# Half of some steps' exponentials on VectorE, in a convolution and attention kernel whose ScalarE and TensorE are both full

## The chip, the cores and the metric

The kernel runs on one core of one Trainium2 chip. A core has five engines that run their own instruction streams in order and meet through semaphores: TensorE (PE in the profile; its weight loads are PEld), VectorE (DVE), ScalarE (ACT), GpSimd (POOL) and SyncE (SP), whose queue issues nearly all DMAs here. The metric is the device time of one execution in microseconds, as the median of several runs. Differences below about 0.2% can't be told from no change.

## What is computed

An image batch of 4 x 64 x 64 x 128 in fp32 goes through two layers. Layer 0 is a gated block: ELU, a 3x3 convolution, a second one with a gate, and a strictly causal attention over the 4096 pixels of an image. Layer 1 is a transformer block on the same 4096 tokens: full attention with 16 heads of 8 channels, a gated feed-forward part, and a mixture of 8 experts of which two are used per token. The part that fills the time is layer 1's attention:

```python
scores = jnp.einsum('bqhd,bkhd->bhqk', q, k)      # 4 images x 16 heads x 4096 x 4096
probs = jax.nn.softmax(scores.astype(jnp.float32), axis=-1).astype(q.dtype)
attn = jnp.einsum('bhqk,bkhd->bqhd', probs, v).reshape(bsz, seqlen, DIM)
```

That is 4 x 16 x 4096 x 4096, or 1.07 billion exponentials. The kernel takes no maximum away before the exponential (it bounds the scores instead, and has a second, general path that runs only where the bound is exceeded); the row sums come from a column of ones beside the values.

## The kernel before, in words

**Attention steps.** Heads are worked on in 4 groups (g) of 4, queries in 8 chunks (c) of 512, keys in 32 tiles (kt) of 128. One `attention_step` (L776) is one group, one query chunk and one key tile. Its first half, `scores()`, puts four matmuls of 512 columns into two PSUM tiles of 1024 (`s`, from a pool of three) and has ScalarE take the exponential of each into an SBUF tile `e` of 1024, from a ring of eight. Its second half, `values(es)`, multiplies the four parts of the two `e` tiles with the values and adds to the one PSUM accumulator `acc`. An image has 4 x 8 x 32 = 1024 such steps, the four images 4096. A `Segment` is a run of key tiles for one group and chunk, mostly all 32; in the first image some are split, so that work may begin while keys are still being made. At a segment's end DVE copies `acc` to SBUF (`at`).

**First steps.** Layer 0's attention uses the same kind of step with two exponentials, `first_step` (L701): 36 an image. Together these are 4240 steps with 8480 exponentials of about 1024 columns.

**Fillers.** Everything else (convolutions, projections, feed-forward, experts) is written as generators that yield after each small piece, with the piece's TensorE time: `first_attention` and `convolutions` for the next image, `second_operands`, and `last_part` after the attention of a chunk. They use one PSUM tile of one bank (`m`, from a pool of one), which DVE empties after each piece.

**Order.** The order of each engine's instructions is the order in which the program writes them: `InOrder` (L91) ties every instruction to the one before it on its engine. The main loop (from L1188) makes one turn per step: it writes the scores of the next step (`do_step`), adds a rate to a credit in microseconds of TensorE, lets one filler piece in while the credit is positive (`insert`), and then writes values until two steps are left undone (`finish(2)`). So the values of a step stand two turns after its scores. The rate is the fillers' remaining TensorE time by the steps left for it. In the first two turns of a segment no filler is let in (`quiet`). Before the loop, `run_alone` works through the first image's preparation, and after it through what is left of the fillers, both with the `s` tiles in place of `m` (`alone`).

All instructions carry the line of the recording helper (L105 before), so the profile is read by the names of the tiles: `s<-qx,f_kx` are a step's scores, `e<-s` an exponential, `acc<-e,vg` values, and `m<-...` fillers.

```python
        credit = min(0.7, credit + rate)
        if waiting or credit > 0.0 and not quiet[0] or urgent and not held[0]:
            credit -= insert()
        finish(2)
```

Of the kernel before, what the change touches and what calls it, by code (L numbers as in the profile page):

```python
# [9 lines left out]
FP = mybir.dt.float32  # L10
FR = mybir.dt.float32r
AF = mybir.ActivationFunctionType
ALU = mybir.AluOpType
AX = mybir.AxisListType

P = 128
C = 128
IMG = 64
N = IMG * IMG
NT = N // P  # L20
QB = 512
# [70 lines left out]
    return np.concatenate(list(parts.values()), axis=1), where  # L92


class InOrder:


    def __init__(self, tc, engine):
        self._tc, self._engine, self._last = tc, engine, None

    def __getattr__(self, name):
        op = getattr(self._engine, name)

        def call(*args, **kw):
            made = op(*args, **kw)  # L105
            if self._last is not None:
                after = mybir.DependencyInfo(mybir.DependencyClass.NoSync, mybir.DependencyReason.DATA)
                self._tc.add_manual_dep(made.ins, self._last, after, reason="as written")
            self._last = made.ins.name
            return made  # L110

        return call
# [3 lines left out]
def fast_path(ctx: ExitStack, tc: tile.TileContext, a: dict, where: dict, out: bass.AP, verdict):  # L116
# [10 lines left out]

    const = ctx.enter_context(tc.tile_pool(name="f_const", bufs=1))
    big = ctx.enter_context(tc.tile_pool(name="f_big", bufs=1))
    ep = ctx.enter_context(tc.tile_pool(name="f_ep", bufs=8))  # L130
    wk = ctx.enter_context(tc.tile_pool(name="f_wk", bufs=2))
    sm = ctx.enter_context(tc.tile_pool(name="f_sm", bufs=2))
    dram = ctx.enter_context(tc.tile_pool(name="f_dram", bufs=2, space=bass.MemoryType.DRAM))
# [15 lines left out]

    def chunk(tag, name=None):  # L150
        return wk.tile([P, QB], FP, tag=tag, bufs=CHUNKS.get(tag, 1), name=name or tag)

    def small(name, dims):
        return sm.tile([P, *dims], FP, tag=name, name=name)
# [64 lines left out]
    seen = const.tile([P, 4, B], FP, name="f_seen")  # L219


    steps_in, undone, fillers, urgent = [], [], [], []
    held, turn = [False], [0]

    def do_step(step):
        scores, values = step
        undone.append((values, scores()))

    def finish(leave):
        while len(undone) > leave:  # L230
            values, es = undone.pop(0)
            values(es)

    def advance(part):

# [67 lines left out]
    def spread(eng, taps, u_all):  # L303
# [22 lines left out]
            yield 0.0, "stop"  # L326
        spread_of.append(u_all)

    def row_terms(band):
        r = wk.tile([P, 4, 8, IMG + 2], FP, tag="r", bufs=1, name="r")  # L330
        for i, (x, y, op) in enumerate(SUMS):
            pool.tensor_tensor(r[:, i], band[:, x : x + 15 : 2, :], band[:, y : y + 15 : 2, :], op)
        return r
# [272 lines left out]
    def second_operands(b, st):  # L606

        c, d = st.second, st.d
        cols = slice(c * QB, (c + 1) * QB)
        if c == 0:  # L610
            tops_of[b] = small("top1", [2, 2, NQ]), small("topv1", [NQ])
        top1, top_v1 = tops_of[b]
        t, at = st.ready[c]
        cols = slice(c * QB, (c + 1) * QB)


        for pair in range(2):
            ps = bank()[:, : 2 * (C + 1)].rearrange("p (k c) -> p k c", k=2)
            for i in range(2):
                k = 2 * pair + i  # L620
                product(ps[:, i, :], at[:, k * P : (k + 1) * P], w3f)
            rs = small("rs0", [2])
            dve.tensor_scalar(rs, ps[:, :, C], 1e-35, None, ALU.add)
            dve.reciprocal(rs, rs)
            for i in range(2):
                tk = by_k(t)[:, 2 * pair + i, :]
                dve.scalar_tensor_tensor(tk, ps[:, i, :C], rs[:, i : i + 1], tk, ALU.mult, ALU.add)
            if pair == 1:
                st.read += 1
            yield 0.46, "stop"  # L630
        h = chunk("h")
        layernorm(t, h)
        for _ in range(2):
            yield 0.0, "stop"
        sp.dma_start(out=d["t"][c], in_=t)
        sp.dma_start(out=d["h"][c], in_=h)
        yield 0.0, "stop"

        ps = bank()
        transposed(h, ps)  # L640
        yT = chunk("yT")
        dve.tensor_copy(yT, ps)
        yield 0.6, "stop"
        def terms(i, w):

            ps = bank()
            yield from halves(ps, w, yT)
            u = chunk("u")
            two = wk.tile([P, 2, QB], FP, tag="two", bufs=1, name="two")
            dve.tensor_copy(u, ps)  # L650
            dve.tensor_copy(two[:, 0, :].bitcast(FR), u)
            dve.tensor_tensor(two[:, 1, :].bitcast(FR), u, two[:, 0, :], ALU.subtract)
            dve.tensor_reduce(top1[:, i, :, c], two, AX.X, ALU.max, apply_absolute_value=True)
            yield 0.46, "stop"
            if i == 0:
                for y in range(2):
                    sp.dma_start(out=d["q"][c][:, y], in_=two)
            else:
                sp.dma_start(out=d["k"][:, :, cols], in_=two)

        yield from terms(0, wq1)

        ps = bank()
        by_g = ps.rearrange("p (g k s) -> p k g s", g=NG1, k=4)
        for k in range(4):
            product(by_g[:, k], yT[:, k * P : (k + 1) * P], wv1)
            if k == 1:
                yield 0.46, "held"
        vc = wk.tile([P, 4 * NH1, 1 + HD1], FP, tag="vc", bufs=1, name="vc")
        pool.memset(vc[:, :, 0:1], 1.0)  # L670
        dve.tensor_copy(vc[:, :, 1:], ps.rearrange("p (f s) -> p f s", s=HD1))
        dve.tensor_reduce(
            top_v1[:, c : c + 1], vc.rearrange("p f s -> p (f s)"), AX.X, ALU.max, apply_absolute_value=True
        )
        yield 0.46, "stop"
        sp.dma_start(
            out=d["v"][:, :, c].rearrange("g p s -> p g s"),
            in_=vc.rearrange("p (g f) s -> p g (f s)", g=NG1),
        )
        yield from terms(1, wk1)  # L680
        if c == NQ - 1:

            tops2, tops = small("tops2", [2, 2]), small("tops", [2])
            dve.tensor_reduce(tops2, top1, AX.X, ALU.max)
            dve.tensor_tensor(tops, tops2[:, :, 0], tops2[:, :, 1], ALU.add)
            s2 = seen[:, 2, b : b + 1]
            dve.tensor_tensor(s2, tops[:, 0:1], tops[:, 1:2], ALU.mult)
            dve.tensor_scalar(s2, s2, 1e30, None, ALU.min)
            dve.tensor_reduce(seen[:, 3, b : b + 1], top_v1, AX.X, ALU.max)
        st.second += 1  # L690
# [10 lines left out]
    def first_step(c, r, qx0, sums, found):  # L701
# [47 lines left out]
                dve.tensor_copy(at, sums[0])  # L749
                found.append(at)  # L750

        return scores, values


    def keys(d, g, quarter, place):
# [17 lines left out]
        )  # L773
        return vg

    def attention_step(b, seg, kt, place, qx, vg, part):  # L776
        g, c = seg.g, seg.c

        def scores():
            ss, es = [s_tile(), s_tile()], []  # L780
            for j in range(NSLOT):
                r = slice(j * SLOT, (j + 1) * SLOT)
                pe.matmul(
                    ss[j // 2][:, (j % 2) * QB : (j % 2 + 1) * QB],
                    lhsT=kx[r, place * P : (place + 1) * P].bitcast(FR),
                    rhs=qx[r, :].bitcast(FR),
                    start=True,
                    stop=True,
                )
            for s in ss:  # L790
                e = e_tile()
                act.activation(e, s, AF.Exp)
                es.append(e)
            return es

        def values(es):
            for j in range(NSLOT):
                pe.matmul(
                    acc[j * SLOT : j * SLOT + 1 + HD1, :],
                    lhsT=vg[:, kt // 4, kt % 4, j, :],  # L800
                    rhs=es[j // 2][:, (j % 2) * QB : (j % 2 + 1) * QB],
                    start=kt == seg.lo,
                    stop=kt == seg.hi - 1,
                )
# [8 lines left out]
                else:  # L813
                    sp.dma_start(out=scratch[b]["p"][g, c], in_=at)

        return scores, values

    def by_token(b, g, c, at):

# [301 lines left out]
    def stream():  # L1121
# [16 lines left out]
        for at, seg in enumerate(plan):  # L1138
# [13 lines left out]
            for kt in range(seg.lo, seg.hi):  # L1152
# [3 lines left out]
                if seg.lo > 0 and kt == seg.lo + 4:  # L1156

                    part.append(chunk("part"))
                    sp.dma_start(out=part[0], in_=scratch[seg.b]["p"][seg.g, seg.c])
                yield attention_step(seg.b, seg, kt, 8 * seg.place(kt // 8) + kt % 8, qx, vg, part)  # L1160
                if follower and follower not in ahead and follower.ready():
                    bring(follower)
                if kt % 8 == 7:
# [24 lines left out]
    credit, waiting = 0.0, False  # L1188
    while True:
        turn[0] += 1  # L1190
        if steps_in:
            do_step(steps_in.pop(0))
        else:
            step = next(steps, False)
            if step is False:
                break
            waiting = step is None
            if waiting:
                finish(0)
            else:  # L1200
                do_step(step)
        b = now[0]
        if batches[b].second == NQ and len(batches) == b + 1 and b + 1 < B:
            Batch(b + 1)
# [3 lines left out]
        if batches[b].second == NQ:  # L1208
            within = steps_left[b] - 40 if b + 1 < B else min(steps_left[b] - 40, 160)
            rate = sum(us for _, us in fillers) / max(1, within)  # L1210
        credit = min(0.7, credit + rate)
        if waiting or credit > 0.0 and not quiet[0] or urgent and not held[0]:
            credit -= insert()
        finish(2)
    finish(0)
    while urgent:
        if held[0]:
# [722 lines left out]
```

## Time and profile before

| | before |
|---|---|
| median of 3 runs | 8293.93 us (8293.24 to 8297.26) |
| the profiled execution | 8302.43 us |
| its span, first to last instruction | 8300.7 us |
| granted TensorE clock, mean | 0.985 |
| TensorE busy (matmuls) | 8073.1 us, 97% |
| ScalarE busy | 7915.4 us, 95% |
| VectorE busy | 2557.3 us, 31% |
| GpSimd busy | 708.5 us, 9% |
| DMA, share of 16 engines | about 11% |
| first and last exponential | 129.5 and 8222.2 us |

A line of the profile's groups has the line, engine and operation, output and input by the program's names, shape, count, then busy time and the mean duration of one, then the idle time of the engine before these instructions and what ended it. Matmuls are pipelined and their ends are modelled, so a busy TensorE is not TensorE at its peak: what it needs is read from the distance between the starts of groups that follow each other without a wait. Likewise an exponential's mean of 1087 ns is longer than the distance between two of them.

### The profile page before, as it was taken

The numbers are of one execution on the slowest core, as the hardware profiler recorded it, in microseconds if no ns is written. First come the engines' busy times: TensorE is split into PE (matmuls) and PEld (weight loads), VectorE is DVE, ScalarE is ACT, GpSimd is POOL, SyncE is SP. The second block draws the span as 40 slices with busy tenths as digits, with TensorE's granted clock in tenths as the row PEclk, the third lists the DMA queues.
The fourth block names the chain that finished last, engine by engine and source line by source line (L and its number), as shares of the span: only waits on it lengthen the run. The fifth ranks groups of instructions, "written<-read, shape, count | busy, mean of one in ns | idle before, by whom it ended". The sixth has DMA issues, their size and how long they took to land.

```text
span 8300.7 us, 173662 instructions
## 1 busy us (share of the span) xinstructions
PE 8073.1 (97%) x73713; PEld 2576.8 (31%) x73713; DVE 2557.3 (31%) x5278; ACT 7915.4 (95%) x8699; POOL 708.5 (9%) x597
## 2 busy tenths in 40 slices
PE   5899999999999999999999999999999999999998
PEld 3223222223333332333333333233333333332333
DVE  7333122223322223333322222333333223221223
ACT  1799999999999999999999999999999999999996
POOL 5101111000000002111000000211000000000000
PEclk7899999999999999999999999999999999999998
DMA  1222001101100001001010000101111111111110
GB/s 56 70 70 66 19 27 36 36 27 49 41 23 14 21 18 32 22 30 47 33 38 11 27 15 19 30 27 39 42 37 40 33 39 42 38 33 34 59 55 30
DMA packets 239541, 295.99 MB, mean 36 GB/s; under 512 B 81731, under 2 KB 153891, under 8 KB 238755
## 3 DMA queue, kind: packets, MB, share of 16 engines
q1 hardware_dynamic: 234739, 283.03, 10.6%
q8 instruction: 580, 9.50, 0.5%
q10 hardware_dynamic: 4016, 1.77, 0.1%
q14 instruction: 206, 1.69, 0.1%
HBM read 185.12 MB, written 99.61 MB: 34 GB/s over the span
## 4 chain that ended last, share of the span: by engine, by line
PE 87%; issue 7%; DVE 3%; ACT 1%; POOL 1%; DMA 1%; SPq 0%; ACTq 0%; POOLq 0%; DVEq 0%
PE acc L105 41%; PE s L105 28%; PE m L105 18%; ACT e L105 1%; DVE h L105 1%; DVE added L105 0%; DMA nt<-d_a 0%; DVE t L105 0%; POOL v L105 0%; DMA f_kx<-d_k 0%; POOL rs L105 0%; DVE two L105 0%; DMA xe<-in_x_dram 0%; DVE at L105 0%; DVE by_e L105 0%
## 5 line engine op out<-in xcount | busy, mean ns | idle before, releaser
L105 ACT ACTIVATE e<-s 128x1024 f32<-128x1024 f32 x8480 | 7842.5, 1087 | 133.4 <-PE s L105 124.3
L105 PE MATMUL acc<-e,vg 128*9 128x512 f32 x32768 | 4337.9, 595 | 1.7 <-DVE at L105 1.7
L105 PE MATMUL s<-qx,f_kx 32*128 32x512 f32 (+1 forms) x16960 | 2817.2, 495 | 46.5 <-ACT e L105 30.9
L105 PEld LDWEIGHTS s<-qx,f_kx 32*128 32x128 f32 (+1 forms) x16960 | 1128.1, 182 | 4046.7 <-ACT e L105 3788.7
L105 PEld LDWEIGHTS acc<-e,vg 128*9 128x9 f32 x32768 | 711.1, 90 | 784.0 <-issue 446.5
L105 PE MATMUL m<-v,f_wino 128*32 128x256 f32 x5328 | 431.5, 397 | 6.0 <-DVE t L105 3.5
L105 DVE TENSOR_TENSOR by_e<-m,gate 128x512 f32<-128x512 f32 x244 | 168.8, 692 | 725.7 <-PE m L105 725.7
L105 POOL TENSOR_TENSOR v<-r 128x1024 f32<-128x1024 f32 x128 | 248.5, 1947 | 1180.2 <-PE m L105 1159.9
L105 POOL TENSOR_TENSOR rs<-ve,f_minus_half 128x4 f32<-128x4 f32 x64 | 65.2, 1019 | 2997.6 <-DVE ve L105 2957.3
L105 PE MATMUL m<-f_we,y2T 128*32 128x256 f32 x3904 | 311.8, 391 | 2.3 <-DVE nt L105 2.3
L105 DVE COPY sd<-m 128x512 f32<-128x512 f32 x166 | 114.9, 692 | 570.8 <-PE m L105 570.8
L105 DVE COPY at<-acc 128x512 f32<-128x512 f32 x130 | 89.9, 692 | 555.8 <-PE acc L105 555.8
L105 DVE TENSOR_REDUCE added<-by_e 128x128 f32<-128x1024 f32 x128 | 255.3, 1995 | 4.4
L105 POOL TENSOR_TENSOR t<-t,h 128x512 f32<-128x512 f32 x32 | 40.9, 1277 | 2443.6 <-DVE h L105 2443.6
L105 PE MATMUL m<-hT,f_fw 128*32 128x256 f32 (+1 forms) x2728 | 236.1, 391 | 0.0
L105 DVE TENSOR_TENSOR t<-m,sums 128x256 f32<-128x256 f32 x126 | 53.5, 425 | 435.1 <-PE m L105 435.1
L105 DVE TENSOR_TENSOR t<-m,t 128x512 f32<-128x512 f32 x62 | 42.9, 692 | 455.6 <-PE m L105 455.6
L105 DVE SCALAR_TENSOR_TENSOR h<-m,h 128x512 f32<-128x512 f32 (+1 forms) x93 | 64.2, 690 | 372.9 <-ACT th L105 249.1
L105 DVE COPY h<-m 128x512 f32<-128x512 f32 (+1 forms) x93 | 64.2, 690 | 317.9 <-PE m L105 317.9
L105 PEld LDWEIGHTS m<-v,f_wino 128*32 128x32 f32 x5328 | 106.6, 109 | 173.5 <-issue 144.6
L105 PE MATMUL m<-e,f_v 128*32 128x512 f32 (+2 forms) x1128 | 152.2, 585 | 0.0
L105 DVE TENSOR_TENSOR e<-e,f_consts 128x128 f32<-128x128 f32 x128 | 30.2, 296 | 321.5 <-ACT e L105 321.5
(259 smaller groups left out, 3775.8 us busy)
## 6 DMA issues: line engine op xcount, KB each, us to landing
f_kx<-d_k SPq DMA_DIRECT2D x139, 512.0 KB, 4.0
qx<-d_q SPq DMA_DIRECT2D x152, 256.0 KB, 2.8
d_q<-two SPq DMA_DIRECT2D x64, 512.0 KB, 3.6
vg<-d_v SPq DMA_DIRECT2D x32, 576.0 KB, 4.2
d_k<-two SPq DMA_DIRECT2D x32, 512.0 KB, 3.4
d_v<-vc SPq DMA_DIRECT2D x32, 288.0 KB, 2.8
xe<-in_x_dram SPq DMA_DIRECT2D x32, 256.0 KB, 2.9
xt<-in_x_dram SPq DMA_DIRECT2D x32, 256.0 KB, 3.7
```

The source lines that it names most:

```text
L105: made = op(*args, **kw)
```

## The change

In some steps, called late here, the second of the two score tiles is not given to ScalarE. DVE takes it out of PSUM as z = s x log2(e) + a shift and makes 2 to that power: in two halves of 512 columns, each by adding a large constant (which leaves the whole part in the low bits), subtracting to get the fraction, a polynomial of degree five in it, a shift of the whole part into the exponent's place, and a product. These are 17 DVE instructions a late step: one of 1024 columns, four of 512 with one tensor, twelve of 512 with two. The first tile's exponential stays on ScalarE. The late step has tiles of its own (`ea`, `z`, `t`, one each; `q` shares the place of `part`), and the ring of `e` goes from eight tiles to six.

A step is late if no other one is in work, its segment begins at key tile 0, and it is the third of the segment's steps or later but not one of the last seven (`2 <= kt <= seg.hi - 8`). The instructions of the polynomial are not written at once. `InOrder` counts an estimated load for DVE (0.15 us and 1.06 ns a column for each instruction), the loop takes 1.84 us from it each turn (0.92 in a late step's), and `settle(1.5)` at the turn's end writes polynomial instructions while the load is under 1.5. The late step's values are written a turn or more after its last polynomial instruction, at the earliest three turns after its scores, in addition to the ordinary values of that turn. Before the last values of a segment all that is left is written at once (`settle(None)`). The credit for fillers gets 0.92 in a late step's turn, and loses 0.97 when its values are written.

To make room, `vc` (values on their way to DRAM) takes the place of `two` in the first image and of `r` (GpSimd's row terms of the convolutions) in the others.

In the built program 307 steps of 4096 are late, so 8173 exponentials are left to ScalarE in the loop. Of the fillers, one more expert round falls after the loop.

```diff
@@ InOrder
+        self.load = 0.0
...
+            sizes = [int(np.prod(ap.shape[1:])) for ap in (*args, *kw.values()) if hasattr(ap, "shape")]
+            self.load += 0.15 + 1.06e-3 * max(sizes, default=0)
@@ fast_path
-    ep = ctx.enter_context(tc.tile_pool(name="f_ep", bufs=8))
+    ep = ctx.enter_context(tc.tile_pool(name="f_ep", bufs=6))
...
     def do_step(step):
-        scores, values = step
-        undone.append((values, scores()))
+        scores, values, late = step
+        es = scores()
+        if late is None:
+            undone.append((values, es))
+        else:
+
+            slow.append((values, es, late, turn[0]))
...
+    def settle(limit):
+
+        if not slow:
+            return 0.0
+        values, es, todo, since = slow[0]
+        if not todo and (limit is None or turn[0] > since + 2):
+            slow.pop(0)
+            values(es)
+            return 0.97
+        while todo and (limit is None or dve.load < limit):
+            todo.pop(0)()
+        if limit is None:
+            return settle(None)
+        return 0.0
+
+    def powers(z):
+
+        todo = []
+        for h in range(2):
+            zh = z[:, h * QB : (h + 1) * QB]
+            t, q = late_tile("t"), chunk("part", "q")
+            todo.append(lambda t=t, zh=zh: dve.tensor_scalar(t, zh, MAGIC, None, ALU.add))
+
+            todo.append(
+                lambda t=t, zh=zh: dve.scalar_tensor_tensor(zh, t, MAGIC, zh, ALU.subtract, ALU.subtract)
+            )
+            todo.append(lambda q=q, zh=zh: dve.scalar_tensor_tensor(q, zh, POLY[4], zh, ALU.add, ALU.mult))
+            for k in (3, 2, 1):
+                todo.append(
+                    lambda q=q, zh=zh, k=k: dve.scalar_tensor_tensor(q, q, POLY[k], zh, ALU.add, ALU.mult)
+                )
+            bits = t.bitcast(mybir.dt.int32)
+            todo.append(lambda bits=bits: dve.tensor_scalar(bits, bits, 23, None, ALU.logical_shift_left))
+            todo.append(
+                lambda t=t, q=q, zh=zh: dve.scalar_tensor_tensor(zh, q, POLY[0], t, ALU.add, ALU.mult)
+            )
+        return todo
@@ second_operands
-        vc = wk.tile([P, 4 * NH1, 1 + HD1], FP, tag="vc", bufs=1, name="vc")
+        room = wk.tile([P, 2 * QB], FP, tag="two", bufs=1, name="vc") if b == 0 else row_tile()
+        vc = room[:, : 4 * NH1 * (1 + HD1)].rearrange("p (f s) -> p f s", s=1 + HD1)
@@ attention_step
+            if late is not None:
+                e, z = late_tile("ea", 1024), late_tile("z", 1024)
+                act.activation(e, ss[0], AF.Exp)
+                dve.tensor_scalar(z, ss[1], LOG2E, SHIFT, ALU.mult, ALU.add)
+                late.extend(powers(z))
+                return [e, z]
...
         def values(es):
+            if kt == seg.hi - 1:
+                settle(None)
@@ stream
+                late = [] if not slow and seg.lo == 0 and 2 <= kt <= seg.hi - 8 else None
@@ main loop
         turn[0] += 1
+        begun, spare = len(slow), 0.0
...
+        if len(slow) > begun:
+            spare = 0.92
+        dve.load = max(0.0, dve.load - 1.84 + spare)
...
-        credit = min(0.7, credit + rate)
+        credit = min(0.7, credit + rate) + spare
         if waiting or credit > 0.0 and not quiet[0] or urgent and not held[0]:
             credit -= insert()
         finish(2)
+        credit -= settle(1.5)
```

## Prediction

> **What bounds the kernel now.** I read the page's busy shares first, then the work by stage, then the order in time within one attention step, then the waits.
>
> ```profile
> span 8300.7 us, 173662 instructions
> PE 8073.1 (97%) x73713; PEld 2576.8 (31%) x73713; DVE 2557.3 (31%) x5278; ACT 7915.4 (95%) x8699; POOL 708.5 (9%) x597
> ...
> L105 ACT ACTIVATE e<-s 128x1024 f32<-128x1024 f32 x8480 | 7842.5, 1087 | 133.4 <-PE s L105 124.3
> L105 DVE COPY at<-acc 128x512 f32<-128x512 f32 x130 | 89.9, 692 | 555.8 <-PE acc L105 555.8
> L105 DVE TENSOR_TENSOR t<-m,sums 128x256 f32<-128x256 f32 x126 | 53.5, 425 | 435.1 <-PE m L105 435.1
> ```
>
> Two engines look full, VectorE (DVE) two thirds idle. Order in time decides between the two. Two stretches (start, length, engine, what):
>
> ```profile
> 4120.70 14.68 ACT L105 ACTIVATE e<-s 128x1024 f32<-128x1024 f32 x16
> ```
>
> ```profile
> 7502.50 0.91 PE L105 MATMUL s<-qx,f_kx 32*128 32x512 f32 x4
> ...
> 7503.33 1.04 PE L105 MATMUL acc<-e,vg 128*9 128x512 f32 x8
> ...
> 7504.31 0.93 PE L105 MATMUL s<-qx,f_kx 32*128 32x512 f32 x4
> ...
> 7508.42 0.51 PE L105 MATMUL s<-qx,f_kx 32*128 32x512 f32 x4
> ...
> 7508.86 0.64 PE L105 MATMUL m<-f_we,y2T 128*32 128x256 f32 x8
> ...
> 7509.31 1.04 PE L105 MATMUL acc<-e,vg 128*9 128x512 f32 x8
> ...
> 7510.29 0.51 PE L105 MATMUL s<-qx,f_kx 32*128 32x512 f32 x4
> ```
>
> Sixteen exponentials in 14.68 us, the last counted at its full 1.087: 15 p + 1.087 = 14.68, so ScalarE's pace is p = 0.906 us, and two are a step: 1.81. At 7502 TensorE's scores are stretched to 0.91 and the next step comes 1.81 later: ScalarE sets this step. At 7508 TensorE is back to back: scores 0.44, a filler matmul group (m) 0.45, values (acc) 0.98, next scores at 1.87: with a filler TensorE sets it, by 0.06; without one it needs 0.44 + 0.98 = 1.42. So its 97% hides slack in each step without a filler, and ScalarE's 95% hides none: 8480 x 0.906 = 7683 us of the 8092 between the first and the last exponential.
>
> ```profile
> 200.00:2000.00 1800.00, 1752.04 (x14928) 530.55 (x14928) 513.01 (x1093) 1717.92 (x1881) 193.93 (x157) 0.97 0.14 46
> 2000.00:4000.00 2000.00, 1984.49 (x18466) 619.48 (x18468) 607.12 (x1263) 1982.19 (x2176) 172.75 (x141) 1.00 0.09 28
> 4000.00:6000.00 2000.00, 1982.47 (x18580) 622.65 (x18572) 619.10 (x1287) 1977.08 (x2172) 170.76 (x139) 1.00 0.09 27
> 6000.00:8222.00 2222.00, 2213.85 (x21220) 702.99 (x21220) 617.00 (x1283) 2207.38 (x2427) 46.58 (x42) 1.00 0.13 41
> ```
>
> (Columns: stretch, length, busy time of PE, PEld, DVE, ACT, POOL, clock, DMA.) From 2000 us on ScalarE is 99% busy throughout: the saving sought is in the right place. DVE is 28 to 31% busy there.
>
> **What the Trainium skill says.** "Perfetto Trace Analysis", Identifying the Most-Contended Engine: matmul busy share is no measure, since matmuls are pipelined. The trace agrees (97% shown, 1.42 of 1.81 us needed). "VectorE: DVE Perf Modes", The perf-mode tier table: fp32 one-tensor operations from SBUF run two elements a cycle, two-tensor ones and PSUM sources one. The trace agrees:
>
> ```profile
> L105 DVE TENSOR_SCALAR f_wino<-e x2: 419/419/419, 30.2 to 59.4; 128x512 f32<-128x512 f32 x2
> ```
>
> ```profile
> L105 DVE SCALAR_TENSOR_TENSOR g0T<-th,h x32: 691/692/693, 2212.4 to 8248.9; 128x512 f32<-128x512 f32 x32
> ```
>
> "Perfetto Trace Analysis", Matmuls, asks that independent groups rotate through PSUM banks so that eviction overlaps; the fillers have one bank (m), which becomes delicate once DVE is busy.
>
> **The change, part by part.** Counts are from the order of the built instructions.
>
> *Removed:* 307 of the loop's 8480 exponentials (one in each of 307 late steps out of 4096), 307 x 0.906 = **-278 us** of ScalarE. The e ring is not the limit: three steps' tiles are six, and the exponentials of a step reuse the tiles of the third step back, whose values matmuls stand before its scores on TensorE anyway. Cost 0; if it did wait, it would be for the 0.2 us between the issue and the end of a matmul group.
>
> *Added on DVE*, per late step: one 1024-wide z from PSUM (692 + 512 x (692 - 425)/256 = 1.23 us), twelve two-tensor operations at 0.692 (8.30), four one-tensor ones at 0.419 (1.68): 11.2 us, about 11.9 with the 0.04 between dependent operations (4004.36 + 0.42 to 4004.82 in the order of time). The integer shift has no row: 0.42 to 0.69, I take 0.42. 307 x 11.2 = 3440, so DVE goes from 2557 to about 6000 us, near 75% of the loop. It fits only because the emission is metered, at a price of 12.3 us a late step (1.24 + 16 x 0.69), so 3% over the real one; but the meter does not see DVE waiting for ScalarE or TensorE.
>
> *TensorE* has the same matmuls, moved. A late step has no values: 0.44, or 0.89 with a filler, against ScalarE's one exponential of 0.91; level. A settling step has two values groups: 0.44 + 0.98 + 0.98 = 2.40, with a filler 2.85, against 1.81. The order has 131 of the first and 176 of the second. Cover: scores have three tiles; when ScalarE leads, TensorE ends a step's scores some 0.25 us after an exponential, with three more (2.72) ahead of ScalarE; less the next half's scores it may be away 2.2 us. Two values and a filler are 2.41: 0.2 uncovered, 176 x 0.2 = **+35**; bounds 0 and 260 (no lead left: 131 x 0.59 + 176 x 1.04).
>
> *The new wait:* TensorE's late values wait for the last polynomial operation. Behind them stand the ordinary values, the next scores, and ScalarE. Within a segment they are emitted a turn after the last operation, so DVE has about 1.8 us: 0. At a segment's end all that is left is emitted at once. Of 108 segment ends with late steps, 59 force 1 to 11 operations, 255 in all; 36 force four or more (219 operations, 0.66 us each: 145 us). Cover each: 1.5 us of DVE time that the turn had free (its 1.84 less some 0.35 of backlog) and 0.8 of TensorE's lead, 36 x 2.3 = 83. **+60**; bounds 15 and 170.
>
> *DVE behind ScalarE:* it waits for tanh results 69 times for 250.6 us and for masked exponentials 35 times for 321.5; polynomial operations now queue behind these, and TensorE behind them. Before, nobody waited for DVE there. About 140 events with the smaller ones, 0.2 us uncovered each: **+30**, bounds 0 and 150.
>
> ```profile
> DVE e L105 <- ACT e L105: 321.5, 35, 16.3
> ...
> DVE h L105 <- ACT th L105: 250.6, 69, 5.1
> ```
>
> *z frees its score tile later* than an exponential would: 1.23 us plus DVE's backlog, against four exponentials (3.6 us) until ScalarE needs it. Covered to a backlog of about 2.2.
>
> *Edits with one answer:* vc in the tile of two (first batch, eight times) waits for the landing of two's DMA (3.6 us) where DVE and POOL stand in order: 0 to 25, I take +5. vc in r's tile: POOL's next row terms wait for a landing of 2.8 us, beside steps that don't need them: 0. One expert round (two by_e of 0.69, one reduction of 1.9, an add) falls behind the loop: +4. SP's queue keeps its order; its issues move by a turn at most.
>
> Sum: -278 + 35 + 60 + 30 + 5 + 4 = -144. The profiled execution took 8302.4, so 8158; the median of the runs lies 8.5 lower: **8150 us**.
>
> **The rivals.**
> *A, TensorE's lead is gone.* Fillers make 1.87-us steps common (2150 in the order), and each shortens the lead by 0.06. If half of the 260 us of the settling steps shows: -278 + 130 + 60 + 30 + 9 = -49, 8245. For it: in 2000 to 6000 TensorE needs about 182 of each 200 us (groups counted at their back-to-back spacing), ScalarE after the change about 187. Against: after settling the credit falls by 0.97 and two or three fillers are skipped.
> *B, slower: the filler bank.* In the order 1130 of the loop's 1997 reads of m on DVE have polynomial operations straight ahead, 2.6 us on average. TensorE rewrites m no sooner than a step (1.87) and its scores (0.44) after the matmul; the metered backlog (up to 1.5 + 0.69, of which 0.9 is worked off meanwhile) and the eviction take 2.0. The margin is 0.3 us; from a lag beyond it each read costs. Loss passes the 144 at 0.13 us a read; at 0.25, 283 us, so 8433. For it: DVE's unmetered waits. Against: a late step starts only after the one before is settled, which drains DVE.
> *C, everything is covered:* -278 + 20 to 30, 8040.
> *D, it does not do what it says:* the instruction order has the 307 exponentials gone, so only as a polynomial that runs at another rate; a shift at 0.69 adds 0.5 us a late step and pushes to A or B.
>
> **How the numbers follow.** Likeliest 0.56 (its own range 8085 to 8230), A 0.20, C 0.13, B 0.11. The range of 8 in 10 reaches over most of C and all of A and leaves B out: 8040 to 8275. 0.2% (17 us) is about what can be told from no change. Faster: 0.55 of the likeliest, 0.17 of A, all of C: 0.85. Same 0.04 (from A). Slower: B; 0.11.
>
> **What would show it.** Right: 8173 exponentials; ScalarE busy near 7640 us and still the fullest; DVE near 6000; TensorE's waits for z at segment ends, some tens of us; z at 1.2 us. Wrong: a sum over 150 us in TensorE's waits for DVE's reads of m (B), ScalarE's waits for scores in settling steps over 100 us (A), or polynomial operations longer than 0.75 us.

## The result, and the profile after

The changed kernel takes 8644.86 us in the median of 4 runs (8625.58 to 8649.15), the kernel before beside it 8294.64. The ratio is 1.042, 95% interval 1.040 to 1.044: slower by 350 us where 144 less was forecast. The median lies far outside the range.

The page of the changed kernel: span, busy times, and three groups (busy and mean ns; then the idle time before them and what ended it).

```profile
span 8641.8 us, 178047 instructions
...
PE 8149.8 (94%) x73689; PEld 2607.1 (30%) x73689; DVE 5940.3 (69%) x10497; ACT 7715.2 (89%) x8392; POOL 757.5 (9%) x597
...
L116 ACT ACTIVATE e<-s 128x1024 f32<-128x1024 f32 x7866 | 7352.8, 1055 | 494.4 <-PE s L116 476.9
...
L116 DVE SCALAR_TENSOR_TENSOR q<-q,z 128x512 f32<-128x512 f32 x1842 | 1339.0, 727 | 50.0
...
L116 DVE TENSOR_SCALAR z<-s 128x1024 f32<-128x1024 f32 x307 | 375.5, 1223 | 317.6 <-PE s L116 305.8
```

The change did what it says: 7866 + 307 exponentials are left to ScalarE, and VectorE (DVE) is busy for 5940 us (some 6000 were forecast). ScalarE fell from 95% to 89% and still no time was won. By stage (columns: stretch, length, busy PE, PEld, DVE, ACT, POOL, clock, DMA share, GB/s):

```profile
2000.00:4000.00 2000.00, 1922.99 (x17617) 601.09 (x17605) 1423.85 (x2493) 1850.31 (x2010) 167.44 (x129) 0.99 0.09 27
4000.00:6000.00 2000.00, 1907.77 (x17667) 598.50 (x17666) 1488.45 (x2576) 1826.60 (x1982) 178.14 (x130) 0.99 0.08 25
```

Before, ScalarE was busy for 1982 and 1977 us of these stretches. Now it stands for 150 to 173, and TensorE for 77 to 92: both wait, so neither is full and they wait for each other. The waits (sum in us, how many, the longest):

```profile
ACT e L116 <- PE s L116: 476.9, 557, 34.1
...
ACT ea L116 <- PE s L116: 154.8, 179, 8.8
...
PEld s L116 <- DVE z L116: 72.3, 80, 1.8
...
PEld acc L116 <- DVE z L116: 67.3, 60, 6.8
```

ScalarE waited 124 us for scores before; now 477 + 155. The idle time of a weight load (PEld) has to be read with care: while values still run, no load is due, so some 0.86 us stand before the loads of most scores, whoever is named behind them. What TensorE itself loses is the idle time of its matmuls (PE). Before scores, 5 us of that end with z. One stretch in order of time shows both places where ScalarE waits (start, length, engine, what; in brackets the idle time before and what ended it):

```profile
7021.33 4.74 ACT L116 ACTIVATE e<-s 128x1024 f32<-128x1024 f32 x5
...
7023.42 0.50 PE L116 MATMUL s<-qx,f_kx 32*128 32x512 f32 x4
...
7023.85 0.43 PE L116 MATMUL m<-f_fw,g2T 88*32 88x128 f32 x8
...
7024.32 1.04 PE L116 MATMUL acc<-e,vg 128*9 128x512 f32 x8
...
7025.18 0.60 PE L116 MATMUL acc<-ea,vg 128*9 128x512 f32 x2
...
7026.15 0.51 PE L116 MATMUL s<-qx,f_kx 32*128 32x512 f32 x4
...
7026.68 1.02 ACT L116 ACTIVATE ea<-s 128x1024 f32<-128x1024 f32 x1 [0.61 <-PE s L116]
...
7026.72 1.23 DVE L116 TENSOR_SCALAR z<-s 128x1024 f32<-128x1024 f32 x1 [4.09 <-PE s L116]
...
7027.75 1.94 ACT L116 ACTIVATE e<-s 128x1024 f32<-128x1024 f32 x2
...
7029.62 0.19 PEld L116 LDWEIGHTS s<-qx,f_kx 32*128 32x128 f32 x4 [0.86 <-DVE z L116]
7029.62 0.51 PE L116 MATMUL s<-qx,f_kx 32*128 32x512 f32 x4
...
7030.22 1.94 ACT L116 ACTIVATE e<-s 128x1024 f32<-128x1024 f32 x2 [0.53 <-PE s L116]
```

The turn from 7023.42 settles a late step: a filler, its own values, and the late ones (two records for each matmul that the kernel writes, here as everywhere in values), 2.73 us from scores to scores. ScalarE has run dry and stands for 0.61. Then comes the next late step: one exponential, then two more, and ScalarE is dry again at 7029.69, since the scores it needs start at 7029.62 and an exponential follows its scores by 0.60.

### The profile page after: what moved, and what is told of

Its sections match the earlier page's. It is cut to its first block, busy times and chain, and to the rows that moved or that the text cites. A ratio compares the mean times of both kernels' runs of the same rounds, so it can differ in the third digit from the quotient of the medians.

```text
span 8641.8 us, 178047 instructions
## 1 busy us (share of the span) xinstructions
PE 8149.8 (94%) x73689; PEld 2607.1 (30%) x73689; DVE 5940.3 (69%) x10497; ACT 7715.2 (89%) x8392; POOL 757.5 (9%) x597
## 5 line engine op out<-in xcount | busy, mean ns | idle before, releaser
L116 ACT ACTIVATE e<-s 128x1024 f32<-128x1024 f32 x7866 | 7352.8, 1055 | 494.4 <-PE s L116 476.9
L116 DVE SCALAR_TENSOR_TENSOR q<-q,z 128x512 f32<-128x512 f32 x1842 | 1339.0, 727 | 50.0
L116 DVE TENSOR_SCALAR z<-s 128x1024 f32<-128x1024 f32 x307 | 375.5, 1223 | 317.6 <-PE s L116 305.8
L116 ACT ACTIVATE ea<-s 128x1024 f32<-128x1024 f32 x307 | 321.7, 1048 | 157.5 <-PE s L116 154.8
L116 DVE SCALAR_TENSOR_TENSOR z<-q,t 128x512 f32<-128x512 f32 x614 | 446.8, 728 | 17.1
L116 DVE SCALAR_TENSOR_TENSOR q<-z 128x512 f32<-128x512 f32 x614 | 445.0, 725 | 17.0
L116 DVE SCALAR_TENSOR_TENSOR z<-t,z 128x512 f32<-128x512 f32 x614 | 441.2, 719 | 16.3
L116 PE MATMUL acc<-z,vg 128*9 128x512 f32 x1228 | 360.9, 596 | 30.2 <-DVE z L116 29.8
L116 PE MATMUL acc<-ea,vg 128*9 128x512 f32 x1228 | 316.3, 593 | 0.0
L116 DVE TENSOR_SCALAR t<-t 128x512 int32<-128x512 int32 x614 | 275.0, 448 | 0.0
```

## The experiments

All are made from the changed kernel; the edits are shown by their main lines. "Order alone" means that DVE still takes z out of PSUM, the values still wait their turns, and the 16 instructions after z do not run. Each ratio is against the kernel before, run beside it.

| run | late steps | median us | ratio, 95% interval |
|---|---|---|---|
| e1_sides | 0 | 8290.60 | 0.9996 (0.9988 to 1.0005) |
| e2_dve_beside | 0 (328 sets on DVE) | 9164.13 | 1.1046 (1.1028 to 1.1065) |
| e3_order_alone | 307 | 8469.81 | 1.0212 (1.0195 to 1.0229) |
| e4_no_filler | 319 | 8708.22 | 1.0500 (1.0483 to 1.0518) |
| e5_dve_clean | 0 (328 sets) | 8410.72 | 1.0139 (1.0123 to 1.0156) |
| e6_order_hold | 315 | 8334.37 | 1.0046 (1.0029 to 1.0063) |
| e7_all_scalar | 307 | 8474.96 | 1.0219 (1.0202 to 1.0236) |
| f1_split | 327 | 8934.37 | 1.0771 (1.0753 to 1.0789) |
| g1_steady_order | 313 | 8317.51 | 1.0029 (1.0017 to 1.0040) |
| g2_steady | 313 | 8577.23 | 1.0346 (1.0329 to 1.0363) |
| g3_steady_hold | 323 | 8402.01 | 1.0130 (1.0114 to 1.0145) |
| e8_short_queue | 0 (125 sets) | 8346.49 | 1.0061 (1.0047 to 1.0075) |
| h1_free_turns | 140 | 8257.78 | 0.9953 (0.9940 to 0.9967) |
| h2_free_poly | 140 | 8377.88 | 1.0099 (1.0084 to 1.0115) |

### Taking the change apart: e1, e2, e3

```diff
# e1: no late step; the ring of six and the moved vc stay
-                late = [] if not slow and seg.lo == 0 and 2 <= kt <= seg.hi - 8 else None
+                late = None
# e2: ScalarE makes both, values on time; DVE's work is used by nobody
-            slow.append((values, es, late, turn[0]))
+            undone.append((values, es))
+            slow.append((None, None, late, turn[0]))
# e3, in powers(): only the load is counted
+            for _ in range(8):
+                todo.append(lambda: setattr(dve, "load", dve.load + 0.15 + 1.06e-3 * QB))
```

> No step is late; the ring of six and the new places of vc stay. Theory P (the time is lost because TensorE's work is uneven from turn to turn: the turn after a late step and the settling turn hold more than ScalarE has ahead) and theory B (DVE's longer queue delays what TensorE waits for, evictions of m above all) both expect the time of the kernel before, 8280 to 8310 us. A third, S (the side edits cost it: six tiles, vc's waits for DMAs), expects 8400 or more.

> ScalarE makes both exponentials of every step and values stand at their usual place; DVE still does the 17 instructions in 328 steps, their result unused. P: 8290 to 8360, since TensorE's order is that of before. B: what DVE's queue costs shows whole, with nothing saved on ScalarE: 8600 to 8900 (the 341 us of the change's loss plus the 278 no longer saved, less what z's own wait was).

> 307 late steps in the same order as in the change, but the 16 polynomial instructions after z are left out (the weights of those halves are then not exponentials); DVE is nearly as free as before. P: ScalarE's waits after late and after settling steps stay, 8500 to 8640. B: 8000 to 8100, the 278 us saved less the predicted TensorE cost.

e1: the side edits cost nothing (2 us less, within the interval). e3: the order alone is 179 us slower than e1, with all of ScalarE's 307 exponentials saved and no polynomial run. So about half of the loss is not DVE's. The polynomial adds 175 (8645 less 8470). e3's own time lies between the ranges of both theories, nearer to P.

e2 missed its purpose. DVE's z and ScalarE's exponential read the same score tile, and in the trace z comes after the exponential:

```profile
DVE z L116 <- ACT e L116: 825.8, 312, 6.6
```

DVE stood behind ScalarE in nearly every set, and TensorE's fillers behind DVE (its matmuls' idle time before fillers that ended with DVE rose from 45 to 570 us). Its 9164 us says nothing about DVE's operations themselves; e5 replaced it.

### DVE's operations without anybody waiting: e5, e8

```diff
# e5, as e2, but z is read from a constant tile in SBUF
-                dve.tensor_scalar(z, ss[1], LOG2E, SHIFT, ALU.mult, ALU.add)
+                for h in range(2):
+                    dve.tensor_scalar(z[:, h * QB : (h + 1) * QB], we_f[:, h * QB : (h + 1) * QB], LOG2E, SHIFT, ALU.mult, ALU.add)
# e8, as e5, with a shorter queue on DVE, and so fewer sets
-        credit -= settle(1.5)
+        credit -= settle(0.4)
```

> As the run in which DVE works beside ScalarE, but the first polynomial instruction reads a constant tile in SBUF instead of the scores, so DVE waits for nobody in these 17 instructions (328 sets, result unused). ScalarE and TensorE have the order of before. Theory R (most of the loss is the order of the change on TensorE and the ring of three score tiles; DVE's queue costs about the 175 us between the change and its order alone): 8400 to 8520. Theory B (the queue on DVE by itself explains the 870 us of the earlier run): 8900 or more.

> DVE's 17 instructions by themselves as in the earlier run with 328 sets, but written only while the estimated load is under 0.4 us and not 1.5, which leaves 125 sets and one or two polynomial instructions ahead of most reads of m. If the cost goes with the number of sets (115 us for 328): 44 us, 8330 to 8345. If it comes from long queues ahead of the reads of m: 10 us or less, 8290 to 8305.

e5 costs 115 us for 328 sets, 0.35 each, with every value on time. The idle time of TensorE's filler matmuls that ended with DVE (the profile's lines `PE m <- DVE`, added up) rises from 45 to 116 us. That is rival B's mechanism, at a fraction of its price.

e8 takes 50 us for 125 sets, 0.40 each, as if the loss went with the number of sets. The order in time says otherwise. Fillers don't wait for DVE more than before (44 us); what is new is this wait, of which e1 has 1.1 us:

```profile
PE acc L116 <- DVE at L116: 41.1, 11, 7.5
```

Nine of the eleven, 40 us, lie before 1800 us, at ends of segments. There all that is left of a set is written at once, DVE's copy of `acc` stands behind it, and the next segment's values behind the copy. Here ten polynomial instructions, from 844.94 on, come just before the copy, and the values wait 6.37 us:

```profile
850.55 0.69 DVE L116 SCALAR_TENSOR_TENSOR z<-q,t 128x512 f32<-128x512 f32 x1
851.16 0.68 DVE L116 COPY at<-acc 128x512 f32<-128x512 f32 x1
...
851.89 1.90 PE L116 MATMUL acc<-e,vg 128*9 128x512 f32 x8 [6.37 <-DVE at L116]
```

From the step that e1 reaches at 1800 us to the last exponential, e8 takes 6 us more than e1, though 102 of its 125 sets run there. With a short queue a set costs next to nothing in that stretch: the loss comes from what stands behind a queue on DVE, at segment ends too, and not from the number of sets as such.

### The order: e7, e6, e4

```diff
# e7, as e3, but ScalarE makes the late half too
-                dve.tensor_scalar(z, ss[1], LOG2E, SHIFT, ALU.mult, ALU.add)
+                act.activation(z, ss[1], AF.Exp)
# e4, the whole change; e6 as e3: no filler in a settling turn or the turn after a late one
+        settles = bool(slow) and not slow[0][2] and turn[0] > slow[0][3] + 2
+        after_late = bool(slow) and turn[0] == slow[0][3] + 1
# e6 only: the credit refills faster, and nothing is held in the last 300 steps
+        credit = min(1.4, credit + 1.15 * rate) + spare
```

> The order alone again, but in the 307 late steps ScalarE makes the second exponential too, so it has 307 x 0.906 = 278 us more work than in the order alone; values stand as late as there. R: the extra exponential fills the window in which ScalarE waited two turns after a late step, so the time does not rise by 278 us, it falls: 8340 to 8440, below the 8470 of the order alone. U: 8470, ScalarE's work does not matter. If ScalarE sets the time: 8750.

> The order alone, without the 16 polynomial instructions, and no filler in a settling turn nor in the turn after a late step (except near the end, so that no more fillers are left over); 315 late steps. R: ScalarE's wait two turns after a late step falls from about 0.8 to 0.25 us and that after a settling turn from 0.6 to 0.3, so 8200 to 8280, faster than before. Theory U (TensorE has no room, wherever the fillers stand): 8400 to 8480.

> The change, but no filler is let in in a settling turn nor in the turn after a late step; 319 late steps. P: ScalarE's wait after a settling turn falls from 0.87 to about 0.45 us, and that two turns after a late step from 0.99 to about 0.5, so 8400 to 8500. B: DVE's load is the same and only its place moves: 8600 to 8700.

e7 is the plainest: ScalarE does 278 us more than in e3, and the time is the same (the intervals overlap). In this order ScalarE's saved time is worth nothing. And e7, which takes nothing off ScalarE, is 180 us slower than before by the order of the late values alone: they leave a turn and come back in another, after which ScalarE waits 0.61 us (table below).

e6 wins back 139 us of e3's 177 (both as differences from before), so holding fillers in these two turns makes the order cheaper: ScalarE's wait after a settling turn falls from 0.61 to 0.35 us. It still missed both theories' ranges. With the polynomial, e4 is slower than the change itself. The fillers held back came due later: e4 runs on for 166 us from the start of its last exponential (the changed kernel 84, before 78.5), and between 6400 and 6600 us the next image was not ready, so that only 119 exponentials ran where about 200 do.

### No doubled values: g1, g2, g3, f1

```diff
# g1 (order alone) and g2 (whole change): one values group every turn
-        credit = min(0.7, credit + rate) + spare
+        credit = min(0.7, credit + rate)
...
-        finish(2)
-        credit -= settle(1.5)
+        ready = bool(slow) and not slow[0][2] and turn[0] > slow[0][3] + 2
+        if ready:
+            settle(1.5)
+        finish(2 - len(slow))
+        if not ready:
+            settle(1.5)
# g3, as g1: no filler in the late turn and the next
+        beside = bool(slow) and turn[0] <= slow[0][3] + 1 and (b + 1 < B or steps_left[b] > 300)
# f1, the whole change: the late step's values in two halves, ea's on time, z's later
+            undone.append((values, [es[0], None]))
+            slow.append((values, [None, es[1]], late, turn[0]))
```

> The order alone once more (16 polynomial instructions left out, 313 late steps), but each turn has one group of values: in a late step's turn the ordinary values stay, in a settling turn the late values take the ordinary ones' place, and the credit is left as before. Theory V (the 178 us of the order alone, and the 278 us of ScalarE that bring nothing there, come from values that leave a turn where TensorE can't use the gap and come back in one where it has no room): 8100 to 8240, faster than before. Theory U (fillers and values leave TensorE no room to follow a faster ScalarE): 8280 to 8310.

> The whole change with its polynomial in that steady order, 313 late steps. V: the steady order alone plus what DVE's queue costs (115 us measured by itself, 175 us between the change and its order): 8250 to 8400, so 250 to 400 below the change. If the polynomial's late end costs more where its values hold an ordinary place: 8500 or more.

> The steady order alone (16 polynomial instructions left out, 323 late steps) with no filler in a late step's turn nor in the one after it. Theory W (after a late step the next scores need a tile that its one exponential frees, so TensorE's part from there, 0.43 + 0.45 + 0.97 + 0.57 = 2.42 us, faces two exponentials, 1.81, and not three): the wait after a late step falls from 0.77 to about 0.4 us, 8210 to 8265, faster than before. U (the fillers' work only moves): 8295 to 8330.

> The whole change with its polynomial, 327 late steps, but the values of a late step are split: the two matmuls on ScalarE's half go with the next ordinary values, the two on DVE's half come when it is ready; no filler in those turns nor in the turn after a late step. R: the order's loss falls to about 200 us, DVE's 175 stay: 8330 to 8430. U: 8600 to 8700.

g1 takes away the settling turn's double load. It wins 153 us against e3 and is still 24 slower than before, though ScalarE has 313 exponentials less; theory V's range is missed, and U's only just. One late step of it, with a filler:

```profile
5041.00 0.77 PE L116 MATMUL s<-qx,f_kx 32*128 32x512 f32 x4
...
5041.70 0.43 PE L116 MATMUL m<-f_fw,g2T 88*32 88x128 f32 x8
...
5042.02 1.03 ACT L116 ACTIVATE ea<-s 128x1024 f32<-128x1024 f32 x1
...
5042.16 1.04 PE L116 MATMUL acc<-e,vg 128*9 128x512 f32 x8
...
5043.13 0.51 PE L116 MATMUL s<-qx,f_kx 32*128 32x512 f32 x4
...
5043.73 1.02 ACT L116 ACTIVATE e<-s 128x1024 f32<-128x1024 f32 x1 [0.68 <-PE s L116]
```

The late exponential starts without a wait and is done at 5043.05. The next scores start only at 5043.13, because the turn still holds scores, filler and values. ScalarE stands for 0.68 of the 0.906 it saved. The same count over all turns, from the starts of exponentials (the distance from a turn's last to the next turn's first, less 0.905, and less 0.53 for another operation between), from 600 us on:

| kernel | wait after a late turn with / without a filler, us | after a settling turn | all turns |
|---|---|---|---|
| before | none | none | 185 |
| e3 (values deferred) | 0.12 (207) / 0.02 (95) | 0.61 (302) | 614 |
| e7 (as e3, ScalarE makes all) | 0.00 (207) / 0.00 (95) | 0.61 (302) | 342 |
| changed kernel | 0.12 (207) / 0.02 (95) | 0.87 (302) | 781 |
| g1 | 0.89 (209) / 0.51 (99) | 0.04 (308) | 469 |
| g3 | 0.90 (56) / 0.49 (263) | 0.11 (319) | 522 |
| h1 | 1.01 (1) / 0.51 (139) | 0.06 (140) | 255 |
| h2 | 1.00 (1) / 0.52 (139) | 0.54 (140) | 372 |

In g1 a late step's saving of 0.906 comes back as 0.89 where the turn has a filler and as 0.51 where it has none: 0.02 or 0.40 is kept. That is 1.81 - 1.42, the room between ScalarE's step and TensorE's turn without a filler, and nothing where the turn has one. Over all turns g1's waits grow by 284 us (469 less 185), as much as its 313 exponentials save: what free turns keep is lost in others. In e3 and the changed kernel the late turn itself has no values, so the wait only moves: two turns later it sums to about 250 us in both, 0.83 for each late step. In e7 that wait is gone.

g3 meant to win this by holding fillers away. Over all late steps the wait fell from 0.77 to 0.56 us (0.4 was expected), but the time rose to 8402: a hole at 6200 to 6400 us with 98 exponentials, in which the next image is made ready, and 122 us from the start of the last one. Held fillers are not gone.

f1 failed mainly in the same way. It holds fillers in still more turns. Between 6400 and 6800 us ScalarE's waits sum to 276 us (36 in the changed kernel), and it runs on for 143 us from its last exponential (84): together 299 us more, against 289 by which f1 is slower than the changed kernel. Besides, splitting a values group saves TensorE no time:

```profile
6308.94 1.03 PE L116 MATMUL acc<-z,vg 128*9 128x512 f32 x4
...
6309.90 0.50 PE L116 MATMUL s<-qx,f_kx 32*128 32x512 f32 x4
```

Two matmuls (four records) take 0.96 us to the next scores, in the median of 311 such groups too, as four do (0.97 in g1 above). So the split gives TensorE about 0.97 x 327 = 317 us more work, an estimate; in ScalarE's waits outside that hole no such loss shows (754 us against 742). Whether this work is part of what pushed fillers into the hole is not separated.

g2 missed theory V's range. Against g1 it has the polynomial's price in this order: 260 us for 313, or 0.83 each. TensorE's settling turns, from scores to scores, grow from 1.79 to 2.45 us in the mean of 308, which is 206 us. The idle time of its filler matmuls that ended with DVE grows from 47 to 96 us. The two together, 255 us, come near the 260, though fillers' waits within settling turns count in both.

### Only where a turn is free: h1, h2

```diff
# both, on top of g1 and g2
-                late = [] if not slow and seg.lo == 0 and 2 <= kt <= seg.hi - 8 else None
+                late = [] if not slow and seg.lo == 0 and 2 <= kt <= seg.hi - 8 and credit + pace[0] <= 0.0 and not urgent else None
...
+        pace[0] = rate
...
+        after_late = bool(slow) and turn[0] == slow[0][3] + 1
+        if waiting or credit > 0.0 and not (quiet[0] or after_late) or urgent and not held[0]:
```

> The late order alone (the 16 polynomial instructions are left out, so these halves are not exponentials), one values group each turn, and only in turns that would get no filler in any case, with no filler in the turn after: 140 late steps. No filler has to give way. Theory X (a saved exponential is worth the gap between ScalarE's 1.81 us and TensorE's 1.42 us of a turn without a filler, and no more): 140 x 0.39 = 55 us less, of which up to 14 us goes back in waits: 8235 to 8255. Theory U (in a late step the ring of three scores tiles hands back the whole exponential, filler or none): 8290 to 8310. If TensorE's own sum decides (the filler that gives way comes back somewhere), also about 8290, but then with a long tail or with more filler beside the other turns.

> The same 140 late steps with the polynomial on VectorE, so all exponentials are made. VectorE's operations cost 0.40 us for each set of two halves when nobody waited for them and 0.57 us for each late step in the whole change. Theory X: the run before it plus 140 x 0.4 to 0.57, that is 8290 to 8335: nothing is gained, nor is it slower than the kernel before by more than half a per cent. If the loss of the change lay in its order only: the same as the run before it within 15 us.

h1 is the one order that wins: 38 us (27 to 50 by its interval), 0.27 for each late step. Its waits, and those of h2:

```profile
ACT e L116 <- PE s L116: 173.6, 252, 35.4
...
PEld s L116 <- DVE z L116: 23.0, 17, 2.1
```

```profile
ACT e L116 <- PE s L116: 264.4, 326, 35.8
...
PEld s L116 <- DVE z L116: 115.6, 125, 2.1
...
PEld acc L116 <- DVE z L116: 67.3, 50, 5.2
...
PE acc L116 <- DVE z L116: 31.4, 20, 4.3
```

The count puts h1's return at 0.51 a late step, so 0.40 x 140 = 55 us are kept around them; 38 arrive, a little short of the 41 to 55 expected, and 17 remain unexplained. That late steps in free turns keep something is shown by h1's time; that one beside a filler keeps nothing rests on the count in g1.

h2 puts the polynomial back: 120 us, 0.86 each, and the win is gone. This exceeds what was expected (0.4 to 0.57). The settling turns show where: ScalarE's wait after them rises from 0.06 to 0.54, 68 us of the 120, and TensorE's, from scores to scores, from 1.72 to 2.30 us, 81 us in sum. In them the late values wait for the last product (31 us on the matmuls; the 67 on the weight loads overlap with these and with running matmuls). Filler matmuls wait 81 us for DVE instead of 44. The line that grows most, weight loads of scores behind z, from 23 to 116 us, is no such loss: z starts 0.22 us after the late exponential in the mean, and 0.23 in h1, and TensorE's own idle time there is 8 us in both. No version tried beats the kernel before with all exponentials made.

## Why the prediction was wrong, by its steps

The forecast lay 495 us too low. The runs divide that as follows: the order's terms (-278 + 35 = -243) measured +179 (e3 less e1), 422 off; DVE's waits (60 + 30) measured +175 (changed kernel less e3), 85 off; the side edits (+9) measured -2.

- **The removed exponentials, -278: the step that failed.** The count, the pace and the place were right, but the term took ScalarE as what sets every step. Beside a filler a turn of TensorE is 1.87, and even a free one is 1.42, so one late step can keep at most 1.81 - 1.42 = 0.39; 207 of the 302 late turns counted have a filler. In the change's order the term measured about 0: e7 has these exponentials back on ScalarE and differs from e3 by 5 us, within the intervals. The best order with as many late steps, g1, has +24 in the place of -278.
- **"Level" for the late step, 0.** TensorE's 0.44 or 0.89 against one exponential was right inside the turn. It left out the turns after it, whose length does not shrink: about 250 us come back two turns later. The stage averages had misled as well: TensorE needing 182 of 200 us seems to leave room, but its lead is three tiles, too short to carry the slack of a free turn to a full one. That the three tiles are the reason is argued from the waits; a fourth tile was not tried.
- **Settling turns, +35, bounds 0 to 260.** Measured: 302 x 0.87 = 262 us of waits in the changed kernel, the upper bound. In time it is 180 us (e7 against before) or 153 (e3 less g1, as the differences from before). The cover of 2.2 us was three exponentials, 2.72, less some 0.5 for the way back to the next scores; from the start of scores to the exponential that waits for them alone the traces have 0.53 and 0.60 (7026.15 to 7026.68, 7029.62 to 7030.22), and the late step at 7026 meets a lead that is still spent. Rival A was this mechanism, with half of the 260; its sign, over 100 us of such waits, is there.
- **DVE's durations** were right: z 1.223 us (1.23 forecast), two-tensor operations 0.727 in the mean of the group shown and 0.692 in its median (0.692), the shift 0.448 (0.42).
- **Segment ends, +60:** the late values' matmuls wait 30 us for z, 21 of it at segment ends, at the low end of 15 to 170. Settling turns as a whole grow from 2.73 us in e3 to 2.99 in the mean, 78 us over all 302; how much of that is the wait for z is not separated.
- **z frees its tile late, covered:** right, with some 5 us of TensorE's own idle time in the changed kernel; the 72 us above are weight loads' idle time.
- **DVE behind ScalarE and the bank of the fillers (rival B).** TensorE's waits for DVE in fillers rose from 45 to 141 us on the matmuls, just short of the 150 named as B's sign (with weight loads, which hold more than stalls, from 152 to 419). In time the whole polynomial is 175, which the two terms for DVE put at 90. B had its sign and its mechanism right in part, but put all of the loss there; half of it was the order.
- **vc, the ring of six:** +9 forecast for the edits, 2 us less measured.

## What to carry to other kernels

Before work is taken off a full engine, ask what the next engine needs in the very turn where the saving falls, not in the stage's average: here, with a ring of three tiles between them, a saving was worth at most the gap of that one turn (0.39 us of 0.906) and nothing where a filler closed it. Run the new order with the added work left out, and the added work with nobody waiting for it: the two runs showed that the change had lost already before the first polynomial. Added work on an idle engine costs by what stands behind its queue: copies at segment ends, evictions, values. Work held back to make room comes due elsewhere, so look at the tail and for holes before a saving is believed.

## What the runs showed of the hardware

**VectorE beside GpSimd.** In the changed kernel, the instructions that write q take 690 ns where no GpSimd operation overlaps them (2091 of them) and 1520 ns in the mean where only a tensor-tensor operation of GpSimd does (104). One line of the tile's list has the spread (min, median, max in ns):

```profile
L116 DVE SCALAR_TENSOR_TENSOR q<-q,z x1842: 668/692/2429, 434.1 to 8556.3; 128x512 f32<-128x512 f32 x185
```

The Trainium skill has the reason ("SBUF — State Buffer", SBUF: two separate sides): VectorE with two SBUF inputs and GpSimd reading SBUF share a pair of ports as an exclusive lock, and the later one is fully blocked. The trace shows it: in 85 of the 86 cases where GpSimd's operation had started first, the VectorE instruction ended 0.55 us after it; in the 33 where VectorE's had, it took its usual 0.68 to 0.69 us. The prediction priced all these operations at 692 ns. The 104 cost some 86 us of VectorE's 5940.

**Half a values group costs a whole one:** 0.96 us for two matmuls into two of the four column groups, 0.97 for four into all four (f1 and g1).

**TensorE after stalls.** Of the 32,792 records of values matmuls (0.59 us in the median, at most 1.06 before), 144 take more than 0.8 us before, 421 in the changed kernel and 1621 in e2, whose mean clock is 0.954. "TensorE: Matmul & The Clock Gate", Part 1: The HAM clock gate, says that the array runs at half its clock after an idle window. The counts go that way; how much of the loss it is was not measured apart. It isn't needed for the order's loss: g1, with 168 such records and before's clock (0.985), keeps nothing of its saving either.
